# Rounding positions in fp16 on ScalarE, evicting table differences there, and giving the last layers layer 0's buffers

## The chip, the cores and the metric

The kernel runs on one core of a Trainium2 chip. The metric is the device time of one execution in microseconds (us); the median of the runs counts. The core has five engines that run side by side: TensorE (PE, matrix multiply, with its weight loads listed as PEld), VectorE (DVE), ScalarE (ACT), GpSimd (POOL) and SyncE (SP), which here issues all the DMAs. Each runs its own list of instructions in the order that was fixed when the program was built, and waits where an operand or a buffer is not ready.

## The reference: four graph layers

Inputs are `x` (16 x 1024 x 64, fp32), a 0/1 adjacency `adj` (16 x 1024 x 1024) and a node mask. Four layers follow, each on `h = relu(layernorm(x))`, and each adds its result to `x`. What matters of them:

```
layer 0:  nb = neighbours without self; m = their number; skip = ceil(m/2) where m > 10
          remove each skip-th neighbour (symmetrically); valid = what is left, with self
          sv = sort of h over the valid neighbours, per node and channel
          for tau, w in (.25,.5,.75),(.25,.5,.25):
              pos = tau*(m-1);  q = sv[floor(pos)]*(1-frac) + sv[ceil(pos)]*frac;  agg += w*q
          x += (relu((h+agg) @ W1 + b1) @ W2 + b2) * mask
layer 1:  A = adj + I;  x += (A @ h) / rowsum(A)
layer 2:  8 heads: x += softmax(g0 * q k^T / 8 + g1 * adj) v @ Wproj + b,   g = exp(h @ Wg + bg)
layer 3:  x += adj @ (h @ W3) + b3
```

## The kernel before

The 16 batch elements b go through a pipeline. Layer 0 of element b runs beside layers 1 to 3 of element b-1; in the background the next element's adjacency is thinned (`dilate`) and, for two elements at a time, all values are ranked with a bitonic sort (`ranks`).

**Layer 0 without gathering.** Every value of a channel has a rank from 0 to 1023, cut into 64 buckets of 16. `group` makes, for four pairs of channels and 512 nodes at a time, three tables by matrix products with `valid`: `cum` (how many valid neighbours lie in the buckets below each bucket; line 694 takes it out of PSUM), and the halves `c1` and `c0` of a bit word of the ranks in the bucket (`pword`, 699 and 704, evicted by ACT as `hi`, 706). The matrix `dif_k` at line 704 takes the difference of `cum` between neighbouring buckets. For each of six positions q (floor and ceil of three quantiles), `compare` (729) finds with `le = cum <= krow[q]` (735) the bucket that holds position k, sums words and table values with `le` (737 to 756), and `bits` and `value` pick the value within it. So `le` depends only on how `cum` and `krow` compare. One step is one q; an element has 96 steps (8 groups x 2 halves x 6).

**Positions.** `positions` (583) counts the valid neighbours of each node into `m1` = m-1 (int16). For each q, DVE works out `tau*m1`, for the odd q plus 3 in units of a quarter, and shifts right by 2 (lines 602 and 603); ACT turns the result into fp16 as `krow[q]` (605). `kq` and `coef` are made in the same way, for all q at once.

**Table.** `sorted_table` (621) transposes the sorted values, takes the difference of neighbouring ones by a product with `tab_d` (637), and DVE evicts it four times per element with a factor by parity (`par`) and `UP` = 4096 into `df` (639 to 642), which is split into two fp16 parts.

**Order.** `picks` (713) issues the steps; `stages` (923) spreads the making of the next element's `valid`, positions and table over the last 12 steps of the present element. After each step, the loop at line 1149 issues as much of `layers()` as is due, .42 units a step against 40.5 units for layers 1 to 3 of an element. When `picks` is through, lines 1153 and 1154 issue the rest of `layers()` alone: what is left of element 14, then layers 1, 2 and 3 of element 15. The scheduler of the framework orders each engine's instructions; `adjoining` keeps some matrix products together.

**Buffers.** PSUM has eight banks of 512 fp32: tags `pa`, `pb` and `pc` have two each (helpers `pa`, `pb`, `pc_`), and the scores `sp` one tile of two. Layers 1 to 3 take everything but the scores from `pb`: transposes `pcols`, outputs `ao`, projections `pp`, keys and queries `pk` and `pq`, layer 1's and 3's `two` and `po`. Layer 0 uses `pa` and `pc`. In SBUF the exponentials `s` are in `b4` (two), transposed rows `eT` and `aT` in `bt` (two, `chunk_cols`, 406), and `kT`, `qT`, `v2` have one buffer each. Layer 0 has `a4` (four), `tb` (six) and `q4` (two).

**Layer 2** (1017) runs over four pairs of heads; each makes `kT`, `qT` and `v2`, then goes over eight blocks of 128 rows: load `ad`, scale it on ACT, scores for two halves of 512 columns (1074), add and running minimum on DVE (1083), exponential with its sum on ACT (1089), sixteen transposes through `pcols` with ACT copies to `eT` (412, 415), outputs (1093), copy `aoT` (1102), projection (1104), and two additions to `xr` on DVE (1106).

**Set-up.** DVE makes the constants first. `rev` holds the bit-reversed numbers 0 to 1023, the same row in all 128 partitions, from 10 masks-and-shifts and 10 ORs (137 and 141); it goes to DRAM as `rev_d` and each ranking loads it at line 528. The scratch pool is closed at line 345, and the main SBUF pool takes its place.

Of the kernel before, what the change touches and what calls it, by code (L numbers as in the profile page):

```python
# [8 lines left out]
F32 = mybir.dt.float32  # L9
# [12 lines left out]
P = 128  # L22
# [7 lines left out]
TOP = 2.0 ** 23  # L30
MID = 1600.0
UP = 4096.0
LOW = 2048.0


@with_exitstack
def tile_preln_adj_stack(
# [44 lines left out]
    def a4(name, shape=(P, N), dt=F32):  # L82
        return sb.tile(list(shape), dt, tag="a4", bufs=4, name=name)
# [11 lines left out]
    def a2(name, shape=(P, 512), dt=F32):  # L95
        return sb.tile(list(shape), dt, tag="a2", bufs=4, name=name)
# [5 lines left out]
        return ps.tile(list(shape), dt, tag="pc", bufs=2, name=name)  # L102


    def b4(name, shape=(P, N), dt=F32):
        return sb.tile(list(shape), dt, tag="b4", bufs=2, name=name)

    def pb(name, shape=(P, 512), dt=F32):
        return ps.tile(list(shape), dt, tag="pb", bufs=2, name=name)

    def small(name, shape, dt=F32, bufs=3):
# [6 lines left out]
    def sc(name, shape=(P, P), dt=F32):  # L118
        return scrp.tile(list(shape), dt, name=name)
# [7 lines left out]
    identh = const.tile([P, P], HP, name="identh")  # L127
    nc.vector.tensor_copy(identh, identf)

    rev_i = sc("rev_i", (P, N), I32)  # L130
    nc.gpsimd.iota(rev_i, pattern=[[1, N]], base=0, channel_multiplier=0)
    rev_a = sc("rev_a", (P, N), I32)
    rev_b = sc("rev_b", (P, N), I32)
    nc.vector.memset(rev_a, 0)
    for b_ in range(N.bit_length() - 1):
        up = N.bit_length() - 2 - 2 * b_
# [2 lines left out]
            op1=OP.logical_shift_left if up >= 0 else OP.logical_shift_right,  # L139
        )  # L140
        nc.vector.tensor_tensor(rev_a, rev_a, rev_b, OP.bitwise_or)
    rev = sc("rev", (P, N), HP)
    nc.vector.tensor_copy(rev, rev_a)
    rev_d = dram.tile([P, N], HP, name="rev_d")
# [26 lines left out]
    par = const.tile([P, 2], F32, name="par")  # L171
    nc.vector.tensor_copy(par[:, 1:2], par_i[:, 0:1])
    nc.vector.tensor_scalar(par[:, 0:1], par[:, 1:2], -1.0, 1.0, op0=OP.mult, op1=OP.add)
    for c2 in range(2):
        cols = slice(c2 * BKW, (c2 + 1) * BKW)
        for i, w in enumerate((1.0, LOW)):
            nc.vector.tensor_scalar(
                sel_w[:, i, cols], fcol_i[:, :BKW], 0.0, w, op0=OP.mult, op1=OP.add
            )
            nc.vector.tensor_scalar(sel_w[:, i, cols], sel_w[:, i, cols], par[:, c2 : c2 + 1], None, op0=OP.mult)  # L180
# [81 lines left out]
    nc.vector.memset(mid_c[:, 0:1], MID)  # L262
    nc.vector.memset(mid_c[:, 1:2], MID * LOW)
    nc.vector.memset(mid_c[:, 2:3], -MID)

    sel_q = const.tile([P, NQ, 2 * BKW], BF, name="sel_q")
    for q in range(NQ):
# [137 lines left out]

    def chunk_cols(ad, name):

        aT = sb.tile([P, C, P], F32, tag="bt", bufs=2, name=name)
        for s in range(2):
            pt = pb("pcols", (P, 4, P))  # L410
            adjoining(
                nc.tensor.transpose(pt[:, c, :], ad[:, (4 * s + c) * P : (4 * s + c + 1) * P], identf)  # L412
                for c in range(4)
            )
            nc.scalar.copy(aT[:, 4 * s : 4 * s + 4, :], pt)  # L415
        return aT
# [65 lines left out]
    def ranks(V):  # L482
# [42 lines left out]
        nc.sync.dma_start(vs, F)  # L525
        yield "half"
        R = b2_("rev", (P, N), HP)
        nc.sync.dma_start(R, rev_d)

        last = (len(steps) - 1) // 4  # L530

# [51 lines left out]
    def positions(valid):  # L583

        m1 = sb.tile([P, N], I16, tag="m1", bufs=1, name="m1")
        for t in range(NH):
            pm = pa("pm")  # L590
            adjoining(
                nc.tensor.matmul(
                    pm, ones, valid[:, j, t * 512 : (t + 1) * 512], start=j == 0, stop=j == C - 1
                )
                for j in range(C)
            )
            nc.vector.tensor_scalar(m1[:, t * 512 : (t + 1) * 512], pm, -1.0, None, op0=OP.add)
# [12 lines left out]
        nc.vector.tensor_scalar(n6, n6, 2, None, op0=OP.logical_shift_right)  # L610
        kq = sb.tile([P, N], HP, tag="kq", bufs=1, name="kq")
        nc.scalar.copy(kq, n6)
        yield krow, kq
        nr = a2("nr", (P, N), I16)
        nc.vector.tensor_scalar(nr, m1, r_tau, None, op0=OP.mult)
        nc.vector.tensor_scalar(nr, nr, 3, None, op0=OP.bitwise_and)
        coef = sb.tile([P, N], BF, tag="coef", bufs=1, name="coef")
        nc.vector.tensor_scalar(coef, nr, w_frac, w_one, op0=OP.mult, op1=OP.add)
        yield coef

    def sorted_table(s, vs):
# [46 lines left out]
    def group(g, t, bk, pw, valid, weights):  # L668
# [16 lines left out]
        for pp in range(4):  # L685
# [5 lines left out]
                nc.tensor.matmul(pc, cw[:, j, :], valid[:, j, hs], start=j == 0, stop=j == C - 1)  # L691
                for j in range(C)
            )
            nc.scalar.copy(cum[:, pp, :], pc)  # L694
            if late is not None:
                low_part(*late)
            pw_ = pc_("pword")
# [319 lines left out]
    def layer2(b, xr):  # L1017
# [17 lines left out]
        HW = H * D  # L1035
        for pr in range(H // 2):

            kT = sb.tile([P, N], F32, tag="kT", bufs=1, name="kT")
            qT = sb.tile([P, N], F32, tag="qT", bufs=1, name="qT")
            v = sb.tile([P, C, P], F32, tag="v2", bufs=1, name="v2")  # L1040
            for t in range(NH):
                hs = slice(t * 512, (t + 1) * 512)
                both = ((kT, slice(0, D), pb("pk")), (qT, slice(D, P), pb("pq")))
# [19 lines left out]
            for i in range(C):  # L1063
# [5 lines left out]
                nms = [None, None]  # L1069
                for t in range(NH):  # L1070
                    hs = slice(t * 512, (t + 1) * 512)
                    sps = ps.tile([P, 2, 512], F32, tag="sp", bufs=1, name="sp")
                    adjoining(
                        nc.tensor.matmul(  # L1074
                            sps[:, e, :], qT[e * D : (e + 1) * D, i * P : (i + 1) * P],
                            kT[e * D : (e + 1) * D, hs], start=True, stop=True,
                        )
                        for e in range(2)
                    )
                    for e in range(2):  # L1080

                        nm = small("nm", [P, 1], bufs=6)
                        nc.vector.tensor_tensor_reduce(  # L1083
                            ss[e][:, hs], sps[:, e, :], ad[:, hs], -1.0, 3.0e38 if t == 0 else nms[e],
                            op0=OP.add, op1=OP.min, accum_out=nm,
                        )
                        nms[e] = nm
# [101 lines left out]
```

## Time and profile before

Three runs took 14,069.84, 14,073.2 and 14,090.67 us: a median of 14,073.2. The profiled execution took 14,083.12 us, 14,080.9 of it from the first to the last instruction (the span).

| what | value |
|---|---|
| busy ACT, its three largest groups | `s` exponentials 1169.9 us, `eT` copies 1110.1, `vs` 927.1 |
| busy DVE, its three largest groups | `wa` 1865.8 us, `wb` 1864.1, `le` 1863.6 |
| mean granted TensorE clock | 0.978 |
| DMA | 838 MB, mean 60 GB/s |
| element's end (`xr<-xr,o`, 972), first and fourteenth | 1098.8 and 12,041.9 us |
| the same, last | 13,653.1 us |

A group's row reads: line, engine, operation, output<-input by the program's names, shapes, count; then its busy time in us and the mean ns of one; then how long its engine stood idle just before, and what ended most of that. A row of waits reads: who waited, for whom, us in total, times, longest.

### The profile page before, as it was taken

How to read it: one execution, taken by the hardware profiler on the slowest of the kernel's cores; microseconds unless marked ns; L12 is line 12 of the kernel's file. 1: busy time of each engine (PE TensorE's matmuls, PEld its weight loads, DVE VectorE, ACT ScalarE, POOL GpSimd, SP SyncE). 2: the span in 40 equal slices, each digit the busy share in tenths (PEclk: the TensorE clock that was granted, in tenths of full speed). 3: DMA queues.
4: the chain of work that ended last, by engine and by line, in shares of the span. 5: the costliest groups of instructions: out<-in, count | busy, mean ns of one | idle time of the engine just before them, and what ended most of it. 6: DMA issues, size and time to landing. Idle time of an engine off the chain costs nothing. (4 is left out here: it accounts for less than half of the span.)

```text
span 14080.9 us, 236134 instructions
## 1 busy us (share of the span) xinstructions
PE 12452.1 (88%) x94402; PEld 5955.5 (42%) x95489; DVE 12849.4 (91%) x23280; ACT 8198.1 (58%) x14170; POOL 25.0 (0%) x138
## 2 busy tenths in 40 slices
PE   1889989999899998999899998998989999999987
PEld 0224444444444444444444444444444444444444
DVE  9999999999999999999999999999989999988863
ACT  1446656566566665656566665665656566665655
POOL 0000000000000000000000000000000000000000
PEclk9999999999999999999999999999999999999999
DMA  3012121211212112121211212122121211202011
GB/s 95 28 35 65 47 82 49 77 55 51 77 47 84 49 55 71 53 79 50 70 57 55 76 49 78 49 66 66 48 76 50 71 61 53 82 25 62 26 58 55
DMA packets 478672, 838.40 MB, mean 60 GB/s; under 512 B 232448, under 2 KB 234624, under 8 KB 477568
## 3 DMA queue, kind: packets, MB, share of 16 engines
q1 hardware_dynamic: 477568, 823.24, 18.8%
q8 instruction: 747, 12.24, 0.4%
q14 instruction: 357, 2.92, 0.1%
HBM read 616.27 MB, written 206.83 MB: 58 GB/s over the span
## 5 line engine op out<-in xcount | busy, mean ns | idle before, releaser
L699 PE MATMUL pword<-valid,dw 128*128 128x512 fp8e4 x8192 | 1985.5, 385 | 141.6 <-DVE dw L665 101.3
L691 PE MATMUL pc<-valid,cw 128*128 128x512 fp8e4 x8192 | 1973.9, 381 | 26.0 <-DVE valid L479 13.9
L737 DVE TENSOR_TENSOR wa<-le,c 128x2048 f16<-128x2048 f16 x1536 | 1865.8, 1215 | 134.8 <-PE prep L751 119.6
L735 DVE TENSOR_TENSOR le<-cum,krow 128x2048 f16<-128x2048 f16 x1536 | 1863.6, 1213 | 16.5 <-PE val L751 16.4
L739 DVE TENSOR_TENSOR wb<-le,c 128x2048 f16<-128x2048 f16 x1536 | 1864.1, 1214 | 3.5 <-PE prep L751 3.3
L362 ACT ACTIVATE s<-s,nm 128x1024 f32<-128x1024 f32 x1024 | 1169.9, 1143 | 728.3 <-DVE nm L1083 727.0
L758 ACT COPY wi<-prep 128x512 f32<-128x512 f32 x1536 | 896.8, 584 | 943.3 <-PE prep L751 796.9
L362 ACT ACTIVATE hi<-pword,mid_c 128x512 f16<-128x512 f32 x1024 | 703.2, 687 | 1140.4 <-PE pword L704 1135.5
L1074 PE MATMUL sp<-kT,qT 64*128 64x512 f32 x4096 | 1168.8, 646 | 200.8 <-DVE nm L1083 192.5
L699 PEld LDWEIGHTS <-dw 128*128 128x128 bf16 x8192 | 763.5, 99 | 1262.6 <-DVE dw L665 228.0
L412 PE MATMUL pcols<-identf,s 128*128 128x128 f32 x8192 | 1156.1, 283 | 155.7 <-ACT s L362 74.7
L691 PEld LDWEIGHTS <-cw 128*128 128x128 bf16 x8192 | 764.5, 98 | 1085.4 <-issue 250.1
L412 PEld LDWEIGHTS pcols<-identf,s 128*128 128x128 f32 x8192 | 913.8, 143 | 627.1 <-ACT eT L415 238.8
L415 ACT COPY eT<-pcols 128x512 f32<-128x512 f32 x2048 | 1110.1, 593 | 85.2 <-PE pcols L412 83.3
L1093 PE MATMUL ao<-eT,v 128*64 128x128 f32 x16384 | 1079.9, 277 | 63.8 <-ACT eT L415 60.7
L751 PE MATMUL val<-le,tab 128*32 128x512 f16 x12288 | 1092.2, 388 | 47.7 <-DVE vs L779 30.4
L779 DVE SCALAR_TENSOR_TENSOR vs<-pz,vs 128x512 f32<-128x512 f32 x1536 | 1045.0, 680 | 65.4 <-PE pv L1057 14.9
L362 ACT ACTIVATE vs<-val 128x512 f32<-128x512 f32 x1536 | 927.1, 604 | 235.7 <-PE val L751 146.3
L1093 PEld LDWEIGHTS ao<-eT,v 128*64 128x64 f32 x16384 | 905.5, 137 | 317.3 <-ACT eT L415 212.6
L694 ACT CAST cum<-pc 128x512 f16<-128x512 f32 x1024 | 603.8, 590 | 719.0 <-PE pc L691 674.7
L751 PE MATMUL prep<-wb,sel_w 128*32 128x512 f16 x6144 | 642.5, 396 | 261.8 <-DVE wb L739 238.5
L362 ACT ACTIVATE c<-pword,mid_c 128x512 f16<-128x512 f32 x1024 | 711.2, 695 | 196.9 <-PE pword L681 182.7
(260 smaller groups left out, 19147.0 us busy)
## 6 DMA issues: line engine op xcount, KB each, us to landing
ad<-in_adj_dram SPq DMA_DIRECT2D x768, 512.0 KB, 3.6
adjT_d<-aT SPq DMA_DIRECT2D x128, 512.0 KB, 4.6
aT<-adjT_d SPq DMA_DIRECT2D x128, 512.0 KB, 3.7
md<-sm SPq DMA_DIRECT2D x216, 256.0 KB, 2.0
sb<-md SPq DMA_DIRECT2D x216, 256.0 KB, 2.9
rem_d<-rem SPq DMA_DIRECT2D x128, 256.0 KB, 2.0
left_d<-left SPq DMA_DIRECT2D x128, 256.0 KB, 2.6
left<-left_d SPq DMA_DIRECT2D x128, 256.0 KB, 3.8
```

Source lines behind the costliest of these rows:

```text
L362: nc.scalar.activation(out_, in_, func, **kw)
L412: nc.tensor.transpose(pt[:, c, :], ad[:, (4 * s + c) * P : (4 * s + c + 1) * P], identf)
L415: nc.scalar.copy(aT[:, 4 * s : 4 * s + 4, :], pt)
L691: nc.tensor.matmul(pc, cw[:, j, :], valid[:, j, hs], start=j == 0, stop=j == C - 1)
L699: nc.tensor.matmul(pw_, dw[:, j, :], valid[:, j, hs], start=j == 0, stop=False, skip_group_check=True)
L735: nc.vector.tensor_tensor(le, cum, bc(el.krow[q][:, None, hs], [P, 4, 512]), OP.is_le)
L737: nc.vector.tensor_tensor(wa, le, c0, OP.mult)
L739: nc.vector.tensor_tensor(wb, le, c1, OP.mult)
L751: nc.tensor.matmul(dst[32 * pp : 32 * pp + 32, :], w[pp], r[pp], start=i in (0, 3), stop=i in (2, 4), tile_position=(0, 32 * pp),)
L779: nc.vector.scalar_tensor_tensor(vs, pz, -191.0, vs, op0=OP.is_equal, op1=OP.mult)
L1074: nc.tensor.matmul(sps[:, e, :], qT[e * D : (e + 1) * D, i * P : (i + 1) * P], kT[e * D : (e + 1) * D, hs], start=True, stop=True,)
L1093: nc.tensor.matmul(ao[e * D : (e + 1) * D, :], v[:, j, e * D : (e + 1) * D], eTs[e][:, j, :], start=j == 0, stop=j == C - 1, tile_position ...
```

## The change

Four edits:

- **Positions.** `krow[q]` is made by one ACT instruction from `m1`: `m1 * tau + 1032 - 0.375` for even q, `+ 0.375` for odd q, written as fp16. From 1024 to 2048 fp16 holds whole numbers only, so the conversion rounds to floor or ceil. `cum` is moved up by the same 1032, by a bias tile. The constant falls out of the differences that `dif_k` takes.
- **Table differences.** ACT evicts `df`, with the factor `par * UP` from a tile `par_up`.
- **Bit reversal.** `rev` is made as 128 x 8, eight numbers a partition, and broadcast to all partitions when it is loaded.
- **The last layers' buffers.** A list `alone` is filled when `picks` is through. From then on `b4` tiles come from `a4`, `pb` tiles other than `pcols` from `pa`, `chunk_cols` writes to `tb`; odd pairs of heads put `kT` and `qT` in `q4` and `v2` in `hT`; and the second half of each block's scores goes to two `pc` banks.

```diff
+BASE = 1032.0
...
+    alone = []
+
     def b4(name, shape=(P, N), dt=F32):
-        return sb.tile(list(shape), dt, tag="b4", bufs=2, name=name)
+        return a4(name, shape, dt) if alone else sb.tile(list(shape), dt, tag="b4", bufs=2, name=name)
 
     def pb(name, shape=(P, 512), dt=F32):
+        if alone and name != "pcols":
+            return pa(name, shape, dt)
         return ps.tile(list(shape), dt, tag="pb", bufs=2, name=name)
...
-    rev_i = sc("rev_i", (P, N), I32)
-    nc.gpsimd.iota(rev_i, pattern=[[1, N]], base=0, channel_multiplier=0)
-    rev_a = sc("rev_a", (P, N), I32)
-    rev_b = sc("rev_b", (P, N), I32)
+    rev_i = sc("rev_i", (P, C), I32)
+    nc.gpsimd.iota(rev_i, pattern=[[1, C]], base=0, channel_multiplier=C)
+    rev_a = sc("rev_a", (P, C), I32)
+    rev_b = sc("rev_b", (P, C), I32)
...
+    par_up = const.tile([P, 2], F32, name="par_up")
+    nc.vector.tensor_scalar(par_up, par, UP, None, op0=OP.mult)
...
+    up_c = const.tile([P, 3], F32, name="up_c")
+    for i, shift in enumerate((-0.375, 0.375, 0.0)):
+        nc.vector.memset(up_c[:, i : i + 1], BASE + shift)
...
-        aT = sb.tile([P, C, P], F32, tag="bt", bufs=2, name=name)
+        aT = (
+            tb(name, (P, C, P), F32) if alone
+            else sb.tile([P, C, P], F32, tag="bt", bufs=2, name=name)
+        )
...
-        nc.sync.dma_start(R, rev_d)
+        nc.sync.dma_start(R, rev_d.rearrange("(o p) c -> o (p c)", o=1).to_broadcast([P, N]))
...
-            n = a2("n", (P, N), I16)
-            nc.vector.tensor_scalar(n, m1, q // 2 + 1.0, 3.0 * (q % 2), op0=OP.mult, op1=OP.add)
-            nc.vector.tensor_scalar(n, n, 2, None, op0=OP.logical_shift_right)
             krow.append(sb.tile([P, N], HP, tag="krow", bufs=NQ, name="krow"))
-            nc.scalar.copy(krow[q], n)
+            act(
+                krow[q], m1, AF.Identity, scale=(q // 2 + 1) / 4.0, bias=up_c[:, q % 2 : q % 2 + 1]
+            )
...
-                nc.vector.tensor_scalar(
-                    df[:, :, c2, :, e], pd[:, :, :, c2].rearrange("p q c -> p c q"),
-                    par[:, c2 : c2 + 1], UP, op0=OP.mult, op1=OP.mult,
+                act(
+                    df[:, :, c2, :, e], pd[:, :, :, c2].rearrange("p q c -> p c q"), AF.Copy,
+                    scale=par_up[:, c2 : c2 + 1],
                 )
...
-            nc.scalar.copy(cum[:, pp, :], pc)
+            act(cum[:, pp, :], pc, AF.Identity, bias=up_c[:, 2:3])
...
-            kT = sb.tile([P, N], F32, tag="kT", bufs=1, name="kT")
-            qT = sb.tile([P, N], F32, tag="qT", bufs=1, name="qT")
-            v = sb.tile([P, C, P], F32, tag="v2", bufs=1, name="v2")
+            if alone and pr % 2:
+                kT, qT = q4("kT"), q4("qT")
+                v = sb.tile([P, C, P], F32, tag="hT", bufs=1, name="v2")
+            else:
...
-                    sps = ps.tile([P, 2, 512], F32, tag="sp", bufs=1, name="sp")
+                    if alone and t % 2:
+                        sps = [pc_("sp") for _ in range(2)]
+                    else:
+                        sp = ps.tile([P, 2, 512], F32, tag="sp", bufs=1, name="sp")
+                        sps = [sp[:, e, :] for e in range(2)]
...
             due -= next(two) or due
+    alone.append(True)
     for _ in two:
         pass
```

More of the change, by code (lines that the diff above doesn't have):

```diff
@@ L141, in tile_preln_adj_stack @@
         nc.vector.tensor_tensor(rev_a, rev_a, rev_b, OP.bitwise_or)
-    rev = sc("rev", (P, N), HP)
+    rev = sc("rev", (P, C), HP)
     nc.vector.tensor_copy(rev, rev_a)
-    rev_d = dram.tile([P, N], HP, name="rev_d")
+    rev_d = dram.tile([P, C], HP, name="rev_d")
     nc.sync.dma_start(rev_d, rev)
@@ L1036, in layer2 @@
         for pr in range(H // 2):
-            kT = sb.tile([P, N], F32, tag="kT", bufs=1, name="kT")
-            qT = sb.tile([P, N], F32, tag="qT", bufs=1, name="qT")
-            v = sb.tile([P, C, P], F32, tag="v2", bufs=1, name="v2")
+            if alone and pr % 2:
+                kT, qT = q4("kT"), q4("qT")
+                v = sb.tile([P, C, P], F32, tag="hT", bufs=1, name="v2")
+            else:
+                kT = sb.tile([P, N], F32, tag="kT", bufs=1, name="kT")
+                qT = sb.tile([P, N], F32, tag="qT", bufs=1, name="qT")
+                v = sb.tile([P, C, P], F32, tag="v2", bufs=1, name="v2")
             for t in range(NH):
@@ L1071, in layer2 @@
                     hs = slice(t * 512, (t + 1) * 512)
-                    sps = ps.tile([P, 2, 512], F32, tag="sp", bufs=1, name="sp")
+                    if alone and t % 2:
[3 more added lines that the diff above has]
+                        sps = [sp[:, e, :] for e in range(2)]
                     adjoining(
                         nc.tensor.matmul(
-                            sps[:, e, :], qT[e * D : (e + 1) * D, i * P : (i + 1) * P],
+                            sps[e], qT[e * D : (e + 1) * D, i * P : (i + 1) * P],
                             kT[e * D : (e + 1) * D, hs], start=True, stop=True,
@@ L1083, in layer2 @@
                         nc.vector.tensor_tensor_reduce(
-                            ss[e][:, hs], sps[:, e, :], ad[:, hs], -1.0, 3.0e38 if t == 0 else nms[e],
+                            ss[e][:, hs], sps[e], ad[:, hs], -1.0, 3.0e38 if t == 0 else nms[e],
                             op0=OP.add, op1=OP.min, accum_out=nm,
```

## The prediction

> **What bounds the kernel now.** I read the page's busy shares first, then the windows view by stage, then the groups and the timeline inside each stage.
>
> ```profile
> PE 12452.1 (88%) x94402; PEld 5955.5 (42%) x95489; DVE 12849.4 (91%) x23280; ACT 8198.1 (58%) x14170; POOL 25.0 (0%) x138
> ```
>
> The shares say "VectorE (DVE), with TensorE (PE) close behind", but they average stages with different limits. The windows view splits them. Its columns are the stretch, its length, then the busy time of PE, weight loads, DVE, ScalarE (ACT) and POOL, then the granted clock, DMA share and GB/s.
>
> ```profile
> 0.00:35.00 35.00, 0.00 (x0) 0.00 (x0) 33.63 (x132) 0.00 (x0) 2.20 (x10) 1.00 0.12 29
> 11950.00:12020.00 70.00, 64.74 (x472) 29.34 (x479) 68.36 (x119) 42.95 (x70) 0.00 (x0) 0.98 0.14 49
> 13820.00:13870.00 50.00, 37.24 (x314) 23.87 (x314) 19.41 (x62) 32.25 (x57) 0.00 (x0) 1.00 0.21 63
> ```
>
> Three stages, three limits. **Set-up** (0 to 35 us): only DVE works. **Main loop** (some 310 to 13,623): the row is the end of an element, where the next one's positions and table are made; DVE is full (68.4 of 70), PE nearly so. **Tail** (13,623 to the end, when only element 15's layers 1 to 3 are left): no engine is full; DVE 39%, ACT 65%, PE 74%. There a chain bounds, and the waits of that same 50 us show it as a ring:
>
> ```profile
> DVE s L1083 <- PE pcols L412: 10.4, 12, 1.8
> ...
> ACT s L362 <- DVE nm L1083: 6.4, 5, 1.6
> ...
> PE sp L1074 <- DVE nm L1083: 6.3, 6, 1.3
> ...
> PE pcols L412 <- ACT eT L415: 4.1, 6, 1.4
> ```
>
> Each engine waits for the next: scores wait until DVE has left their only two banks, and the transposes (pcols), outputs (ao) and projections (pp) pass through one pair of banks.
>
> **Part 1: bit-reversal row on 8 columns instead of 1024.**
>
> ```profile
> L141 DVE TENSOR_TENSOR rev_a<-rev_a,rev_b 128x1024 int32<-128x1024 int32 x10 | 12.1, 1214 | 0.0
> L137 DVE TENSOR_SCALAR rev_b<-rev_i 128x1024 int32<-128x1024 int32 x10 | 6.8, 676 | 0.0
> ```
>
> By start-to-start in the timeline these are 10 x 1.14 and 10 x 0.60 us; with the memset (0.9) and the cast (0.6), 18.9 us go. Their 8-column successors are like the 128x1 and 128x8 rows nearby, 0.07 to 0.19 us apart: 22 make some 2.5 with the added constants. Nothing covers this stretch (DVE 96% busy, the other engines empty), and the loads of `x` and `adj` are issued only when the scratch pool is free (35.0). So **-16.5 us**. What could be late next is the weight loads, but SyncE has issued them all by 8.9. The row itself is now broadcast from one 2 KB row in memory rather than read from 128; before shows 3.4 us per load, 8 of them. Twice that on all would be 27 us of latency, of which only the first (at some 200 us, DVE waiting) has no cover: 0 to +3, taken as 0.
>
> **Part 2: positions and table differences leave DVE.** Per element twelve int16 TENSOR_SCALARs go (mean 416 ns; back to back 0.335 apart) and four `df` evictions (473; 0.41 apart): 12 x 0.335 + 4 x 0.41 = 5.7 us, over 16 elements **91 us of DVE**. What is it worth? One bound is all of it, as DVE is full at that place. The other is from elements with less DVE work:
>
> ```profile
> 11203.70:12041.90 838.20, 771.02 (x5917) 368.69 (x5985) 783.38 (x1453) 511.33 (x884) 1.21 (x8) 0.99 0.20 61
> 12041.90:12862.30 820.40, 766.90 (x5868) 367.08 (x5935) 703.50 (x1227) 508.34 (x884) 1.49 (x8) 0.99 0.17 51
> ```
>
> The second has no ranking beside it: DVE -79.9 us, time only -17.8, or 0.22 per us, because PE comes up next (93% busy). The ranking is spread over the element, though, while these 5.7 us sit where DVE is saturated. I take 0.6: **-55**, ends -20 and -91.
>
> ACT pays. `cum` turns from a copy into an activation with a bias tile:
>
> ```profile
> L694 ACT CAST cum<-pc 128x512 f16<-128x512 f32 x1024 | 603.8, 590 | 719.0 <-PE pc L691 674.7
> L362 ACT ACTIVATE hi<-pword,mid_c 128x512 f16<-128x512 f32 x1024 | 703.2, 687 | 1140.4 <-PE pword L704 1135.5
> ```
>
> `hi` is the same shape with a bias: +97 ns x 1024 = 99 us. `krow`, 1049 as a cast, goes by the `cumn` row (1024 wide, bias tile, 1147): +98 ns x 96 = 9. An ACT `df` of 256 columns is not in the trace; between its copies of 128 (268) and 512 (585) lie 374, plus 97 for the scale tile, 471 ns x 64 = 30. Together **+139 us of ACT**, 1.0% of the span on an engine at 58%. Both idle fields are waits for PE, and ACT arrives first, so the longer `cum` delays only what reads it. Its reader L704 stands behind eight pword matmuls and waited 0.3 us in all; bank reuse at L699 waited 16.0. Behind a `df` waiting for its matmul on ACT stand `wi`, `vs` and the layer-2 exponentials, and PE waits for those. If a tenth comes through, **+14**; ends 0 and +139.
>
> **Part 3: the tail gets layer 0's buffers.** Nothing is added; instructions move. In the built order TensorE's stream for one row block i becomes: transposes of head 0 of i, projection of i-1, first half of the scores of i+2, transposes of head 1 of i, outputs of i with the second half of those scores. Scores now run two blocks ahead, and ao and pp no longer share banks with the transposes.
>
> Now: outputs of the second head pair begin at 13816.71 and 13877.34, seven steps, **8.66 us a block**. After, work per block from start-to-start times at full clock: ACT 2.33 (two exponentials with their sums) + 4 x 0.535 (eT) + 1.06 (ad) + 0.24 (aoT) = 5.77; PE 16 x 0.107 + 32 x 0.054 + 2 x 0.87 + 0.3 = 5.5; DVE 3.5. Walking once round the new order, ACT stands still only some 0.13 (first eT behind its transpose), so 5.9. The hand walk leaves out part of the semaphore delays; I take **6.3**, ends 5.9 and 7.8 (half of today's excess over ACT's work stays). Seven steps x 2.36 = 16.5 us. The fill of a head pair (18.3 us from pk to the first outputs) loses about 2, as the second half of the scores no longer waits for DVE. Four pairs: 4 x 18.5 = **-74**; ends -32 and -85. Double kT, qT and v buy little: in the built order pk still stands behind the last pp. `adj` loads land in 3.6 us with three buffers and are issued over a block ahead: hidden at 6.3 too.
>
> The Trainium skill speaks against this part. "TensorE: Matmul & The Clock Gate", section "A second HAM failure mode: psum-queue depth-cycling", says that cycling through PSUM banks can leave so many small PE idles that the clock swings between half and full. By the row, the present cycling already idles PE a quarter of the time and has clock 1.00 (13820 to 13870): gain 74. By the rule, half clock for, say, half the blocks would make PE's 5.5 us 11 there, and the mean with 6.3 is 8.65: only the fill's 8 us would be won. I follow the row, as idle shrinks.
>
> A second rule of that page ("HAM oscillation") wants no PE idle over about 3.4 us. Layers 3 and 1 at the start of the tail say otherwise:
>
> ```profile
> 13655.00:13670.00 15.00, 12.76 (x90) 10.32 (x91) 3.70 (x13) 2.16 (x7) 0.00 (x0) 0.50 0.42 137
> ...
> 13680.00:13690.00 10.00, 7.80 (x81) 5.82 (x80) 4.55 (x23) 6.96 (x16) 0.45 (x3) 1.00 0.90 311
> ```
>
> The clock is 0.50 with gaps of 0.42 us, so by the rule layer 3 would already be warm, with nothing to win. By the row a few of its 3.01 us steps may come near 2.2 when transposes of layer 1 stand between. Layer 1 itself moves 1 MB per 3.29 us at a DMA share of 0.90, and cannot go much faster; the first two blocks' transposes (2 x 1.85 us) do move forward. **-6**, ends 0 and -12. Element 15's own layer 3 keeps its order and its two banks: 0.
>
> **Sum.** -16.5 - 55 + 14 - 74 - 6 = -137.5. Against the profiled execution's 14,083.1 (span 14,080.9 and 2.2 around it) that is 13,945.6. It lies 9.9 above the median of the runs, inside their spread (14,069.8 to 14,090.7); I correct for half and forecast **13,940**.
>
> **Rivals.**
> - *The main loop keeps its time* (0.20). For: the slope 0.22; PE at 93% beside DVE. Against: saturation just there. Set-up and tail alone: 14,078 - 96.5, with nothing net from the loop: **13,982**.
> - *The tail stays a ring* (0.13). For: exponentials, transposes and copies of one block still depend on one another, in a fixed order; against: scores two blocks ahead. At 7.8 us a block, -32 instead of -74: **13,983**, but with the loop faster and the tail not.
> - *ACT becomes what PE waits for* (0.04), the other side. Place: the `cum` to pword link and the `df` evictions at the element's end. For: PE already waits some 300 us for ACT over the run (eT, exponentials, aoT). Against: the idle fields above. Price: all 139 us, with no gain on DVE: 14,078 - 96.5 + 139 = **14,120**. It decides from about 97 us, seven tenths of the added work, landing on the path.
> - *It nets to nothing* (0.03). The builder reorders the loop on every engine, and some 100 us could go that way; before's elements differ by 11 us among themselves: **14,070**.
>
> The forecast holds 0.60. The range reaches from the tail at 5.9 and all of DVE's 91 us (another -47, 13,893), a little more for layers 1 and 3, to the first two rivals with some 20 us more of ACT's work: **13,885 to 14,005**. A measurement of this kernel tells about 0.2% (28 us) from no change. Faster by that: 0.92; within: 0.045; slower: 0.035.
>
> **What would show it.** Part 1: first exchange of the ranking at some 37 us instead of 54.0. Part 2: L602/L603 gone, ACT busy up by some 139 us, elements (mean of the 13 between the first and the fourteenth leave) at 839 rather than 842. Part 3: outputs of successive blocks 6.3 us apart, 63 us a head pair instead of 81.5, ACT above 85% busy there with clock 1.00. Wrong if elements grow longer, if L704 shows waits for `cum`, or if the blocks stay above 8.

## The result, and the profile after

The changed kernel takes **13,959.2 us** (median; 13,949.3 to 13,964.1), the kernel before, run beside it on the same chip, 14,075.3. The ratio is 0.9916, with a 95% interval of 0.9901 to 0.9932. The profiled execution took 13,959.45 us, 13,957.3 of it the span: 123.6 us under the span of before. The forecast was 13,940, with a sum of -137.5 against the profiled execution.

The page's busy shares hardly differ from those of before, which is why the stages have to be read one by one (PE's 121 us more can't be read as work: the page of before has 1,087 fewer matmul records beside the same number of weight loads):

```profile
PE 12573.2 (90%) x95489; PEld 5960.9 (43%) x95489; DVE 12746.0 (91%) x23028; ACT 8308.5 (60%) x14234; POOL 24.1 (0%) x138
```

The windows view of the changed kernel shows set-up, the end of an element of layer 0 (the same stretch before its last addition as before), and two blocks of the last layer 2:

```profile
0.00:35.00 35.00, 0.88 (x3) 0.61 (x4) 29.42 (x194) 4.24 (x6) 1.50 (x11) 1.00 0.38 97
11892.40:11962.40 70.00, 64.38 (x460) 29.60 (x460) 65.04 (x105) 46.36 (x76) 0.00 (x0) 0.98 0.11 35
13744.57:13759.00 14.43, 13.88 (x118) 9.12 (x120) 6.68 (x22) 11.60 (x21) 0.00 (x0) 1.00 0.26 74
```

At the element's end DVE fell from 68.4 of 70 us to 65.0 and ACT rose from 43.0 to 46.4. In the tail's two blocks PE stands at 96% and ACT at 80%, where the 50 us of before had 74% and 65%; the clock is 1.00 in both. The time by stage, from the starts of the same instructions in both traces:

| stage | before | after | difference | predicted |
|---|---|---|---|---|
| first exchange of the ranking (`sm<-sv`), at | 53.98 | 37.19 | -16.8 | -16.5 |
| last leave of layer 0 (`xr<-xr,o`), at | 13,653.1 | 13,592.0 | -61.1 in all, so -44.3 for the loop | -41 |
| from there to layer 2's first transpose | 52.8 | 51.8 | -1.0 | -6 |
| layer 2 of element 15 | 341.0 | 279.4 | -61.6 | -74 |
| the last layer 3 | 34.05 | 34.07 | 0 | 0 |

ACT's own rows in the changed kernel, by the groups view, are the price of the second edit:

```profile
L374 ACT ACTIVATE cum<-pc,up_c 128x512 f16<-128x512 f32 x1024 | 709.2, 693 | 719.2 <-PE pc L706 681.5 <-DVE le L750 26.4 <-DVE bit L781 8.6
...
L374 ACT ACTIVATE krow<-m,up_c 128x1024 f16<-128x1024 int16 x96 | 110.2, 1155 | 27.6 <-DVE le L750 19.5 <-DVE m L612 8.1
...
L374 ACT ACTIVATE df<-pd,par_up 128x256 f32<-128x256 f32 x64 | 27.1, 501 | 5.9 <-PE pd L652 5.9
```

Against before, that is 105.4 + 9.8 + 27.1 = 142 us of instruction time (139 was predicted), though ACT's busy time rose by only 110 (8198.1 to 8308.5): the records of neighbouring ACT instructions overlap, and busy time counts an overlap once (in the last timeline below, 13,740.21 + 1.15 is past the next start, 13,741.27).

**A new ring in the tail.** In the middle of a head pair a block takes 7.45 us. The projections of the second pair start 6.48, four times 7.45, 5.14 and 3.96 us apart; in the last steps of a pair no scores of later blocks are left to make. The 8.66 us of before is a mean over all seven steps, from the first outputs of a pair to the last. The same two places in the changed kernel are

```profile
13737.09 1.96 PE L1116 MATMUL ao<-eT,v 128*64 128x128 f32 x30
...
13783.93 2.12 PE L1116 MATMUL ao<-eT,v 128*64 128x128 f32 x32
```

which makes 46.84 us, or 6.69 a step, where 6.3 had been forecast. The waits of four blocks of the changed kernel (who waited, for whom, us in total, times, longest) show what is left in the middle of the pair:

```profile
DVE s L1106 <- PE sp L1097: 4.7, 8, 0.7
...
ACT s L374 <- DVE nm L1106: 3.4, 3, 1.3
...
ACT ad L374 <- DMA ad<-in_adj_dram: 2.8, 4, 0.8
PEld pp L1127 <- ACT aoT L1125: 2.6, 4, 0.8
```

The timeline of one of these blocks has them in their order (start, length, engine, line, operation, and in brackets the idle time before it with what ended it):

```profile
13752.43 1.15 ACT L374 ACTIVATE s<-s,nm 128x1024 f32<-128x1024 f32 x1 [1.01 <-DVE nm L1106]
...
13753.07 0.33 SPq L435 DMA_DIRECT2D ad<-in_adj_dram  x1
...
13754.71 0.24 ACT L1125 COPY aoT<-ao 128x128 f32<-128x128 f32 x1
...
13755.01 0.49 PE L1127 MATMUL pp<-wproj,aoT 128*128 128x128 f32 x2 [0.55 <-ACT aoT L1125]
13755.42 1.13 PE L1097 MATMUL sp<-kT,qT 64*128 64x512 f32 x4
...
13756.49 1.09 PE L427 MATMUL pcols<-identf,s 128*128 128x128 f32 x8
...
13756.71 1.15 ACT L374 ACTIVATE ad<-ad,gm 128x1024 f32<-128x1024 f32 x1 [0.79 <-DMA ad<-in_adj_dram]
...
13757.87 1.13 PE L1097 MATMUL sp<-kT,qT 64*128 64x512 f32 x4
...
13759.71 0.75 DVE L1106 CUSTOM_DVE_ANT_0 s<-sp,ad,nm 128x512 f32<-128x512 f32 x1
13759.89 1.15 ACT L374 ACTIVATE s<-s,nm 128x1024 f32<-128x1024 f32 x1 [1.06 <-DVE nm L1106]
```

From one exponential to the next, 7.46 us: the two exponentials hold `aoT` back on ACT; the projection `pp` waits for `aoT`; the first half of the scores stands behind `pp` on PE; the second half stands behind head 1's transposes and the first of the outputs; the minimum on DVE waits for the second half; and the next exponential waits for that. The scores do run two blocks ahead of the outputs, but so do the exponentials that need them: in ACT's order the exponential of block i+2 stands right after the copies of block i. So the scores have no lead over their own reader.

### The profile page after: what moved, and what is told of

Read it like the earlier page. It is cut to its first block, busy times and chain, and to the rows that moved or that the text cites. A ratio compares the mean times of both kernels' runs of the same rounds, so it can differ in the third digit from the quotient of the medians.

```text
span 13957.3 us, 237054 instructions
## 1 busy us (share of the span) xinstructions
PE 12573.2 (90%) x95489; PEld 5960.9 (43%) x95489; DVE 12746.0 (91%) x23028; ACT 8308.5 (60%) x14234; POOL 24.1 (0%) x138
## 4 chain that ended last, share of the span: by engine, by line
DVE 28%; PE 25%; ACT 5%; issue 3%; DMA 1%; SPq 0%; DVEq 0%; ACTq 0%
DVE wa L752 4%; PE pword L714 4%; DVE wb L754 4%; DVE le L750 3%; DVE s L1106 3%; PE ao L1116 3%; PE pc L706 3%; ACT s L374 2%; PE pcols L427 2%; PE prep L766 2%; DVE vs L794 2%; PE agg L800 2%; PE sp L1097 1%; DVE bit L781 1%; PE val L766 1%
## 5 line engine op out<-in xcount | busy, mean ns | idle before, releaser
L374 ACT ACTIVATE cum<-pc,up_c 128x512 f16<-128x512 f32 x1024 | 709.2, 693 | 719.2 <-PE pc L706 681.5
```

The source lines that it names most:

```text
L374: nc.scalar.activation(out_, in_, func, **kw)
```

## The experiments

Times are compared with runs of the kernel before on the same chip; "last leave" is read as in the table above. Two traces with the same main loop (before and the first experiment) differ by 4.8 us at that point, and the six traces that have the changed kernel's loop by 11.3 (13,592.0 to 13,603.3), which is the grain of this reading. Layer 2 in the old buffers took 341.0 us in the trace of before, but 336.6 to 338.4 in three others, so the tail's gain is 57 to 62 us.

**The parts alone.** First the tail. The edit is the list `alone` and all that asks for it, put into the kernel before:

```diff
+    alone.append(True)
     for _ in two:
         pass
```

> The kernel before with the buffers of the last layers alone (layer 0's buffers for element 15's last layers; no bit reversal, no table, no positions). If the gains of the change are separate terms, layer 2 of element 15 falls from 341 to about 279 us and the stretch between the last leave and layer 2 by about 1, so the time falls by about 63 us (ratio 0.9955), the elements keep their period of 841.8 and the first exchange stays at 54.0. Rival: the tail gained partly because VectorE and ScalarE were unburdened by the other edits; then layer 2 falls by less than 50 here. Second rival: the buffers cost the main loop something (the period moves by more than 0.5 us per element).

14,020.7 us against 14,073.9, 53 us less, ratio 0.9958 (0.9943 to 0.9973). Layer 2 took 279.45 us, the stretch ahead of it 52.8, the first exchange was at 54.0, and between the first and fourteenth leave the elements took 842.2. The tail's gain doesn't depend on the other edits and costs the loop nothing that shows.

Then the two edits on DVE's work, each alone: the table differences,

```diff
-                nc.vector.tensor_scalar(
-                    df[:, :, c2, :, e], pd[:, :, :, c2].rearrange("p q c -> p c q"),
-                    par[:, c2 : c2 + 1], UP, op0=OP.mult, op1=OP.mult,
+                act(
+                    df[:, :, c2, :, e], pd[:, :, :, c2].rearrange("p q c -> p c q"), AF.Copy,
+                    scale=par_up[:, c2 : c2 + 1],
```

> The kernel before with the eviction of the table differences on ScalarE alone. VectorE loses four evictions of 0.41 us an element, 26 us in all, ScalarE gains some 30. Theory (the work sits where VectorE is saturated, and is worth 0.6 of itself; a tenth of ScalarE's comes through): 13 us less, last leave of layer 0 at about 13,640 instead of 13,653. Rival one (0.22 of VectorE's work, as between two elements of the kernel before): 3 us less. Rival two (the four evictions on ScalarE stand in front of work that PE waits for): 5 us or more longer.

and the positions with the bias on the counts:

```diff
-            nc.vector.tensor_scalar(n, m1, q // 2 + 1.0, 3.0 * (q % 2), op0=OP.mult, op1=OP.add)
-            nc.vector.tensor_scalar(n, n, 2, None, op0=OP.logical_shift_right)
-            nc.scalar.copy(krow[q], n)
+            act(
+                krow[q], m1, AF.Identity, scale=(q // 2 + 1) / 4.0, bias=up_c[:, q % 2 : q % 2 + 1]
+            )
...
-            nc.scalar.copy(cum[:, pp, :], pc)
+            act(cum[:, pp, :], pc, AF.Identity, bias=up_c[:, 2:3])
```

> The kernel before with the positions rounded by ScalarE alone, and with the bias on the cumulated counts that this needs. VectorE loses twelve instructions an element (64 us in all), ScalarE gains 103 ns on each of 1024 evictions and some 9 us on the positions. Theory: 28 us less (39 won from VectorE, 11 lost to ScalarE), last leave at about 13,625 instead of 13,653. Rival one (the slope of 0.22): 14 won, 11 lost, no change within 5 us. Rival two (ScalarE's work is nearly free, so that the whole net gain of 44 us of the changed kernel's main loop is this edit's): 35 us less or more.

| edit alone | median | before | ratio (95%) | last leave | DVE busy, difference |
|---|---|---|---|---|---|
| table differences | 14,049.8 | 14,073.0 | 0.9981 (0.9973 to 0.9989) | 13,624.0 | -22.8 |
| positions and bias | 14,044.3 | 14,073.0 | 0.9977 (0.9968 to 0.9987) | 13,611.8 | -59.6 |
| bias on the counts | 14,074.0 | 14,073.0 | 0.9999 (0.9990 to 1.0007) | 13,656.6 | +4.1 |

The four evictions an element are worth about all of their DVE time (23 us by the medians, where 26 us of start-to-start time went), which none of the expectations had; the interval, 15 to 38 us, leaves out the 13 of the theory only just. The twelve position instructions won 29 us (18 to 45), as forecast. The two alone make 52 us by the medians, or 70 by the last leaves (-29.1 and -41.3); together, in the changed kernel, the medians give 38 and the last leave 44. So the gains may not add, and with both DVE no longer fills that stretch (65.0 of 70). That isn't shown, though: the medians' intervals are wide enough for both sums, the last leaves have the grain above, and each of these kernels has its loop built in another order, which no run takes apart from the work itself.

**What ACT's work costs.** The third row of the table is the longer eviction of the counts, with a bias tile of zeros and nothing else:

```diff
-            nc.scalar.copy(cum[:, pp, :], pc)
+            act(cum[:, pp, :], pc, AF.Identity, bias=up_c[:, 2:3])
```

> The kernel before with the eviction of the cumulated counts made by an activation with a bias tile of zeros, and no other edit: 1024 evictions 103 ns longer each, 105 us more of ScalarE, nothing taken from VectorE. Theory (a tenth comes through): 10 us longer, last leave at about 13,663. Rival one (ScalarE arrives first everywhere): within 3 us of before. Rival two (the eviction stands between the counts and the bit words that PE makes from them): 50 us or more longer.

No change can be seen; the interval of -14 to +10 us excludes that half of the 105 us comes through, but cannot tell 10 from nothing. The other direction is the changed kernel with its constants as numbers in the instruction:

```diff
-            act(cum[:, pp, :], pc, AF.Identity, bias=up_c[:, 2:3])
+            act(cum[:, pp, :], pc, AF.Copy, bias=BASE)
```

(and in the same way for `krow`)

> The changed kernel with its two constants (for the positions and for the cumulated counts) given as numbers of a copy activation instead of bias tiles. If the pointer to the bias tile is what lengthened the eviction from 590 to 693 ns, the eviction falls back to about 600 ns, ScalarE's busy time by about 100 us, and by the tenth of it the time by 10 us against the changed kernel. Rival one: the eviction's length comes from the activation itself and not from the tile, so it stays at about 690 ns and nothing changes. Rival two: the eviction falls back and nothing is won, as ScalarE arrives first.

```profile
L374 ACT ACTIVATE cum<-pc 128x512 f16<-128x512 f32 x1024 | 616.3, 602 | 734.3 <-PE pc L706 690.9 <-DVE le L750 33.5 <-DVE bit L781 4.9
```

The groups view of that kernel has the eviction at 602 ns instead of 693: it was the pointer to the tile, 91 ns, and not the addition, which both have. (The function's name changed too, from Identity to Copy; no run changes that alone.) The Trainium skill agrees ("ScalarE: Activation LUTs", section "What ACT_TABLE_LOAD costs": about 93 ns for each pointer operand). ACT's busy time fell by 91 us and the median to 13,951.6, ratio 0.9911 (0.9898 to 0.9925): 8 us under the changed kernel, too little for the intervals. By the last leave, the three traces with numbers lie at 13,581.7, 13,582.4 and 13,587.3, the six with bias tiles between 13,592.0 and 13,603.3. The ranges don't meet and their means are 12 us apart, about a tenth of ACT's added work. But the loop's built order differs as well (on DVE from about 320 us on), so the 12 us can't be put down to ACT's work alone. The waits that the prediction named as its sign say that little comes through at the eviction itself: for the bank that `cum` frees PE waited 17.0 us in all in the changed kernel, 16.0 before, and the product with `dif_k`, which reads `cum` (now line 719), waited for it 0.3 us before and not at all in the changed kernel.

**The ring in the tail.** If it is as read above, the second half of the scores must leave its place behind head 1's transposes. All four score matmuls of a block are issued together, in the changed kernel:

```diff
+                if alone:
+                    sp = ps.tile([P, 2, 512], F32, tag="sp", bufs=1, name="sp")
+                    made = [[sp[:, e, :] for e in range(2)], [pc_("sp") for _ in range(2)]]
+                    adjoining(
+                        nc.tensor.matmul(
+                            made[t][e], qT[e * D : (e + 1) * D, i * P : (i + 1) * P],
+                            kT[e * D : (e + 1) * D, t * 512 : (t + 1) * 512], start=True, stop=True,
+                        )
+                        for t in range(NH) for e in range(2)
+                    )
```

> The changed kernel, with the four score matmuls of a block of the last layer 2 issued one after the other, before the transposes of the block at hand, instead of two and two with a head's transposes between. Ring theory: in the changed kernel a block of the tail takes 7.45 us because the scores of block i+2 are followed by the row maximum and the exponential of the same block i+2 on one chain, and the second half of the scores stands behind head 1's transposes (1.0 us) and the first product (0.36); together they leave the ring: a block takes 6.0 to 6.2 us, a head pair about 55 us instead of 64.7, layer 2 about 241 instead of 279.4, the time about 38 us less than the changed kernel's 13,959 (about 13,921, ratio to before 0.989). Rival, that PE or ScalarE sets the pace by its own work: the block stays over 7.2 us and the time within 8 us of the changed kernel's.

The time was 13,976.0 us, ratio 0.9930 (0.9914 to 0.9947), and layer 2 took 285.3 us instead of 279.4: nothing gained. The blocks in the middle of a pair did get shorter, 6.1 and 7.4 us in turn with a mean of 6.8 (13,690.30 to 13,703.93 for two) instead of 7.45, so the ring was there. But the same edit made the builder, the scheduler that orders the instructions, arrange the start of each head pair otherwise. ACT's timeline there, after the keys of the second head pair:

```profile
13738.41 1.14 ACT L374 ACTIVATE ad<-ad,gm 128x1024 f32<-128x1024 f32 x1
13740.21 1.15 ACT L374 ACTIVATE ad<-ad,gm 128x1024 f32<-128x1024 f32 x1 [0.66 <-DMA ad<-in_adj_dram]
13741.27 1.05 ACT L430 COPY eT<-pcols 128x512 f32<-128x512 f32 x2
```

Two scalings, one of them waiting for its row, now stand before the copies of head 1 of the first block, which the first outputs need. The main run of these outputs starts 17.0 us after the head pair's first `pv` (13,727.76 to 13,744.71); in the changed kernel it was 11.3 (13,725.81 to 13,737.09). What the seven steps won (42.0 us instead of 46.8, 13,744.71 to 13,786.71), the start lost.

Is ACT's work the limit? The scaling of the rows is left out for the last layer 2:

```diff
-                act(ad, ad, AF.Copy, scale=gm[:, i, 1:2])
+                if not alone:
+                    act(ad, ad, AF.Copy, scale=gm[:, i, 1:2])
```

> The changed kernel without ScalarE's scaling of the adjacency rows in the last layer 2 of element 15 (its factor g1 on the adjacency is left out there: 1.06 us of ScalarE a block). Ring theory: ScalarE's work isn't what a block lasts, so a block stays at 7.45 us within 0.2 and the time within 6 us of the changed kernel's. ScalarE theory: a block falls by the 1.06 us of the scaling, to about 6.4, layer 2 by about 30, the time to about 13,929.

13,972.1 us, ratio 0.9924 (0.9909 to 0.9939). Two blocks took 14.95 us, 7.47 each, with ACT busy for 8.7 of them. The number is that of the ring theory, but the test isn't clean: the builder now put the blocks in twos, their outputs 5 and 10 us apart, and layer 2 took 290.3. It shows that less work on ACT bought nothing in the order that the builder then made, not why.

**The rows' transfers.** ACT also waits for a row of the adjacency in each block. More buffers should tell whether that is on the ring: the two of `b4`, idle in the tail, are added for some rows.

```diff
-        ad = sb.tile([P, N], F32, tag="adj", bufs=3, name="ad")
+        if alone and c % 5 > 2:
+            ad = sb.tile([P, N], F32, tag="b4", bufs=2, name="ad")
+        else:
+            ad = sb.tile([P, N], F32, tag="adj", bufs=3, name="ad")
```

> The changed kernel, with the adjacency rows of the last layers in five buffers instead of three (the two of b4 are free then), so that their loads start two blocks earlier. In the changed kernel ScalarE stands 0.5 to 0.85 us a block before the scaling of such a row. If the ring runs through ScalarE's exponentials, the projection, the scores behind it and head 1's transposes, this wait isn't on it: a block stays at 7.45 us within 0.2, layer 2 at 279 within 5. If the transfer is on the ring, a block falls by 0.5 to 0.85 us to 6.6 to 6.9, layer 2 by 15 to 24.

13,967.5 us, ratio 0.9922 (0.9907 to 0.9936), a block 7.46 us, layer 2 280.9. The wait of ACT didn't shrink, though: 2.8 us in four blocks as before. The premise failed, and the run says nothing of the transfer. The same with the scores together:

> The changed kernel with both: the four score matmuls of a block together, and five buffers for the adjacency rows. With the scores together alone, the blocks alternated between 6.1 and 7.4 us, ScalarE waiting up to 0.9 us for the transfer of a row, and the first outputs of a head pair came 17 us after its values instead of 11. If two rings of nearly the same length held the tail (scores and transfers), both together give 6.0 to 6.3 us a block and 56 to 59 us a head pair, layer 2 about 250 instead of 279, the time about 30 us under the changed kernel's. If it is ScalarE's and PE's own order, a block stays at 6.8 or more and the head pair at 64 to 66.

13,967.3 us, ratio 0.9922 (0.9908 to 0.9937): two blocks 13.56 us, layer 2 279.2, rows still waited for. With the constants in the instruction beside it:

> The kernel of the run before this one, with the two constants as numbers of a copy activation instead of bias tiles. If the two gains are separate, it is 8 to 12 us under that kernel (the profiled execution of the changed kernel with the constants was 12 us under the changed kernel's, its eviction 602 ns instead of 693), so about 13,920. If what the constants won was chance, it equals the run before within 5 us.

13,955.6, ratio 0.9916 (0.9899 to 0.9932), 11.7 us under the run before it, though the slowest of its four executions (13,975.2) is above all of that run's. In the traces the last leave is earlier (13,587.3 instead of 13,597.6) and layer 2 is 3 us longer (282.2). Last, the five buffers strictly in turn (`len(alone)` counts the rows loaded in the tail):

```diff
-        if alone and c % 5 > 2:
+        if alone:
+            alone.append(c)
+        if len(alone) % 5 > 2:
```

> The kernel of the run before (scores together, constants as numbers), with the five buffers of the adjacency rows now used strictly in turn. In the two runs with five buffers ScalarE still waited 0.6 to 0.8 us for a row, since the two added buffers were only given to the rows of blocks 3 and 4 and six rows in a row shared the other three; so those runs didn't take the transfer away. Transfer theory: with the buffers in turn ScalarE waits for no row, every block takes the 6.1 us in which PE works without a gap instead of 6.1 and 7.4 in turn, a head pair 60 us or less, layer 2 about 255 instead of 279 to 282, the time about 20 us under the changed kernel's with the constants, some 13,935. Rival, that PE and ScalarE wait for one another in their own orders: blocks go on alternating at a mean of 6.7 or more though no row is waited for, and layer 2 stays over 270.

13,943.9 us, ratio 0.9908 (0.9891 to 0.9924), the lowest median of all, but the tail had no part in it: layer 2 took 281.1 us. The rival's pace held. The windows view of this kernel has two blocks of the second head pair and two of the last one:

```profile
13737.81:13751.31 13.50, 12.68 (x116) 8.97 (x115) 6.96 (x22) 11.15 (x20) 0.00 (x0) 1.00 0.26 79
...
13876.35:13889.22 12.87, 12.87 (x118) 9.17 (x117) 6.95 (x22) 9.22 (x19) 0.00 (x0) 1.00 0.01 1
```

In the first, a row was still waited for, 0.62 us in two blocks. The order of the instructions explains it: with three buffers a row is loaded and scaled two blocks ahead of its use, with five four blocks ahead. In both its load starts when DVE has read the row whose buffer it takes (13,740.02 in this kernel), and the scaling follows 3.5 us later, as soon as the row has landed. The builder moved the scaling up with the load, and the wait moved along. In the second, no row is loaded or scaled any more (DMA share 0.01), and a block takes 6.43 us with PE busy all the time. So PE's own work, with the scores together, is about 6.4 us a block; rows, their scaling on ACT included, add 0.3. No transfer was fully taken off the ring, so its share is bounded by that 0.3 and not measured by itself. The rest of layer 2 is the starts of the head pairs, as in the run with the scores together alone.

**Layers 3 and 1 at the start of the tail.** There the own buffers won 1 us of 6. One line of the changed kernel's windows view lies in layer 3 of element 14; the second fence is its DMA view (count, KB each, median us to landing) for the stretch between last leave and layer 2:

```profile
13600.00:13615.00 15.00, 12.10 (x87) 9.54 (x83) 0.89 (x4) 1.33 (x5) 0.00 (x0) 0.50 0.72 235
```

```profile
adjT_d<-aT SPq DMA_DIRECT2D x8, 512.0 KB, 4.3
ad<-in_adj_dram SPq DMA_DIRECT2D x7, 512.0 KB, 5.0
aT<-adjT_d SPq DMA_DIRECT2D x6, 512.0 KB, 4.5
```

In the kernel before, the same three landed in 3.1, 4.5 and 3.6 us. Element 14's layer 3 now shares the memory with element 15's layer 1, and PE waits 3.8 us for `aT` (0.9 before). The test puts layer 1's transposed rows back in the two shared buffers:

```diff
-            tb(name, (P, C, P), F32) if alone
+            tb(name, (P, C, P), F32) if alone and name != "aT1"
```

> The changed kernel with the transposed adjacency of the last layer 1 put back in the two shared buffers, all else of the last layers in layer 0's buffers. Contention theory: layer 1's early transfers only delayed layer 3's loads of the same stretch, so the stretch from the last leave to the first transpose of layer 2 stays at 51 to 54 us (51.8 in the changed kernel, 52.8 before), PE's waits for layer 3's loads shrink from 3.8 us to under 2, and layer 2 keeps 279. Rival: the own buffers won what was predicted, 6 us, and something else took 5 back; then this stretch grows to 57 us or more.

One execution, 13,960.1 us: the stretch took 51.1 us, layer 2 279.4. So the buffers bought layer 1 nothing that shows. That they took from layer 3's loads what they gave is shown only in part: PE waited 1.8 us for `aT` instead of 3.8, and `adjT_d` and `ad` landed in 3.2 and 4.4 us again, but `aT` still took 4.4, and PE waited longer elsewhere (3.8 us for `aoT` instead of 2.9, 2.3 for scaled rows instead of 1.6).

## Why the prediction was right, and where it wasn't

**Set-up**: -16.8 against -16.5. Its reason, that nothing covers this stretch, holds, and the broadcast row costs nothing that shows.

**DVE's relief and ACT's work**: "I take 0.6: -55" and "if a tenth comes through, +14" make -41; the trace has -44.3, and the medians, after set-up and layer 2 are taken off their -116, -38. The sum held; its two terms are less sure. By the medians the table's evictions were worth 0.9 of their 26 us and the positions, bias included, 0.45 of their 64, but a slope of 0.6 is inside both intervals. For ACT's tenth, the bias alone cost between -14 and +10 us, and the constants in the instruction won some 12 by the traces, in another built order. The element's period was 838.85 us where 839 had been named.

**The tail**: -61.6 against -74. Layer 0's buffers did break the old ring, alone and in the whole. Counted as the prediction counted, from a pair's first `pk` to its first outputs and from there seven steps to its last, the four fills took 64.5 us instead of 71.4 (7 won, 8 forecast) and the 28 steps 188.1 instead of 241.4 (53 won, 66 forecast): a step fell from 8.62 to 6.72 us in the mean, not to 6.3. The second and third pair took 64.7 us each, where 63 had been named.

The step that failed is the hand walk: "ACT stands still only some 0.13". In the middle of a pair ACT stands 1.0 to 1.3 us for the minimum in most blocks and 0.5 to 0.85 for a row, since the exponentials run ahead by the same two blocks as the scores. Three things were missed. PE's work was put at 5.5 us from spacings within groups of equal matmuls; in a block where PE never rests it is 6.4, and the trace has 0.17 us of issue time at the changes from one kind to the next, which the spacings leave out. The prediction's own row of before said so: 37.24 us busy in 50 at 8.66 us a block are 6.45. The place of a projection between two halves of scores was taken as order only, where it is a link from ACT back to PE. And the rows' loads, "issued over a block ahead" of their use, are not hidden: in ACT's order the scaling comes due before the row has landed (load 13,753.07, scaling 13,756.71 above), and in the second head pair of before ACT had already waited 2.6 us for rows.

That the mean came as near to 6.3 as 6.7 is in part luck: the short steps at the end of a pair, which the walk didn't count, make up for the 7.45 of the ring, which it didn't see. The rival "the tail stays a ring" had the mechanism right; its size, -32, was too pessimistic, since at most four of a pair's seven steps go at the ring's pace.

**Layers 3 and 1**: "-6" was -1.0. The price left out is on layer 3: its loads landed in 4.5 us instead of 3.6, and PE waited 3.8 us for them instead of 0.9. Which of the moved transfers did that stays open, as these loads took 4.4 us with layer 1 back in its two buffers too. The clock of 0.50 stayed, as the row of before had it and against the rule of idle gaps (the Trainium skill, "TensorE: Matmul & The Clock Gate", section "HAM oscillation — how this bites in real kernels"): the row of 13,600 to 13,615 above has it at 0.50 with no wait of PE over 1.7 us.

**The rivals.** The main loop won 38 to 44 us net, so the first is out. ACT as the bound is out by the loop's gain, and the run with the bias alone, whose interval ends at +10 us of the 105, agrees. Under the fourth, one reading was off: the thirteen elements of before between the first and the fourteenth leave differ by 28 us among themselves (833.4 to 861.5), not by 11. The rule on cycling through PSUM banks (same page, section "A second HAM failure mode: psum-queue depth-cycling"), which spoke against the tail, didn't bite here: more banks in rotation, clock 1.00, PE at 96%.

Beyond the change, the lowest medians are those of the kernels with the constants in the instruction (13,951.6, and 13,943.9 with the rows in turn). Their intervals hold the changed kernel's ratio of 0.9916, so the times don't set them apart.

## What to carry to other kernels

Buffers break a ring only as far as the built order lets them: before giving stages a lead, look whether the reader of what runs ahead runs ahead by just as much, and count each engine's work from one block's start to the next where that engine never rests. More buffers for a transfer don't remove a wait when the builder moves the reader up with the load; check in the trace that the wait is gone before the run is taken as a test of it. Compare a mean with a mean: the pace in the middle of a pipeline is not that of its ends. And learn the grain of a reading from traces of the same code before a difference is read from it: six traces of one loop lay 11 us apart here.

## What the runs showed of the hardware that was not expected

- A bias from a tile instead of a number lengthens an activation of 128x512 from 602 to 693 ns, and a copy activation takes a number as its bias.
- TensorE's granted clock stayed at 0.50 for 15 us in which PE was busy for 12.1 (13,600 to 13,615); no run here isolated the cause.
- Three kinds of 512 KB transfers landed 0.5 to 1.2 us later each in the changed kernel's stretch ahead of layer 2 than in that of before (231 GB/s in the mean there instead of 214); one run put two of the three back and not the third.
